# A gated attention block on one core: the main pass's transfers put in written order, the ratios stored in sorted order, and another order of steps in front of the loop

## The chip, the cores and the metric

The kernel runs on one core of one Trainium2 chip. Its time is the device time of one execution in microseconds (us); lower is better. The core has five engines with an instruction queue each: TensorE (PE in the profile; its weight loads are PEld), VectorE (DVE), ScalarE (ACT), GpSimd (POOL) and SyncE (SP). In this kernel SP issues nearly all transfers between memory and the core and does nothing else; what the page calls SPq is SP issuing or waiting.

## What is computed

32 sequences `x` of 256 tokens by 256 channels attend to 32 contexts of 77 tokens, and a feed-forward stage with its own attention follows. All in float32. Cut to what matters:

```python
def proj(t):                                  # layer norm, then 8 heads of 128 features
    return (layer_norm(t, ln_g, ln_b) @ w_in.T) -> [head, batch, token, 128]
f_q, f_k = proj(_layernorm(x)), proj(ctx)     # f_v == f_k
cosine   = f_q . f_k / (|f_q| |f_k|)
q_ratio  = 2 min(var f_q, 1) / (var f_q + 1)  # one number per query and head; k_ratio alike
decorr   = exp(-5 |offdiag(cov f_q)| / D^2)   # one number per head, over all batches
cw, vw, ww = softmax(small_mlp(mean f_q, mean f_k))     # per head, over all batches
mixed    = cw*cosine + vw*decorr*cosine + ww*q_ratio*k_ratio
x = x + tanh(g_xattn) * (mixed @ f_v) @ w_out.T
x = x + tanh(g_ffn)   * ffn(_layernorm(x))    # 16 heads, softmax over the queries, two l2 norms, gelu
```

The weights `cw`, `vw`, `ww` and `decorr` of a head need a pass over all the inputs before the first output can be made.

## The kernel before, in words

**Three stretches.** A first pass reads all inputs once for the statistics that the heads' weights need (up to about 70 us in the profile). A stretch in front of the loop makes the heads' weights and the attention of batches 0 and 1 (to about 150 us). Then a loop, written out in Python for 32 batches, does the rest. In it the list `cycle` (L1470) names what one iteration n does: an entry `(ahead, stage, ...)` runs that stage for batch n + ahead. Batches are in flight up to four ahead: batch n is in its feed-forward attention (`scores`, `exponents`, `mix_values`), batch n + 1 gets its cross attention (`query_scores`, `attend`), batch n + 2 its query features and their transposes, batch n + 3 its inputs' norm and its key features, batch n + 4 is loaded. The last two iterations have lists of their own (`last_but_one`, `last`).

**Orders.** PE, ACT, DVE and POOL are wrapped in `InOrder` (L24 to L32): their instructions run in the order in which the code is written, and every one of them bears line 32 in the profile. The transfers are `nc.sync.dma_start` without the wrapper: their place in SP's queue isn't written down but chosen when the program is built, by a scheduler that plays the program through with estimated times. Once built the order is fixed, and SP runs it in order: a transfer whose input isn't there holds up all that are behind it.

**Turning by way of memory.** From batch 2 on, transposes of 32x32 blocks are made by DVE, and the blocks are put in their places by a store to memory and four reads. So a tile has a store and later reads that must wait for its landing. The pairs of one iteration, with the names that the profile uses:

- queries: `turn_queries` (L583) stores `fd<-fb`, 512 KB for each of two halves t; `fetch_queries` (L592) reads `fqT<-fd` in four parts of 128 KB each. `fqT` has one buffer; PE's `query_scores` (`mm<-fqT,fvT`) needs all eight parts.
- keys: `align_keys` (L337, L341) copies the 77 rows of a batch out of the ring `fvx` into `fv`, in 3 to 5 transfers that depend on where the batch falls in the ring's tiles of 128 rows; `turn_keys` (L407) makes `kb` from `fv` on DVE and stores `kd<-kb`; `fetch_keys` (L416) reads `fvT<-kd`.
- inputs: `transpose_inputs` stores `xd<-xb` (L244) and reads `xq<-xd` four times (L246), one right after the other in the code.
- norms of the keys: `align_norms` copies `nr<-nrx` (L359), stores `nd<-nr` in three parts (L363, L367); `fetch_norms` (L375) reads `rows<-nd`, which POOL's `weigh_keys` turns into `wr`.
- ratios of the queries: `spread_ratios` transposes 128x32 numbers into `rb` on DVE and stores `rc<-rb` (L480, 16 KB); `sort_ratios` (L485) copies `rd<-rc` in memory, in another order (8 KB); `fetch_ratios` spreads `rd` over rows: `re<-rd` (L494) and twice `rqr<-rd` (L503, 256 KB each) with `first`, later `rqr<-re` (L508). POOL's `weigh_ratios` multiplies five blocks of 128x256 of `rqr`, four with a multiply alone and the fifth with a multiply and an add, and DVE adds them to the scores (`s<-mm,wr,rqr`).

Other transfers of an iteration: the load of x (L213), `ff_keep`, which stores `z_kept<-zT` (L799) and `x_kept<-x` (L800) for a repair pass that these inputs don't enter, and the output (`out_dram<-x`, L873, in `ff_add`).

`fb`, the buffer of the transposed queries, and `kb` share two buffers in turn. `keep_running(n)` is n matmuls of 128x128 by 256 columns whose result nobody reads.

Of the kernel before, what the change touches and what calls it, by code (L numbers as in the profile page):

```python
# [15 lines left out]
H = 8  # L16
# [19 lines left out]
def gated_block_kernel(  # L36
# [41 lines left out]

    pe, act, dve, pool = (
# [15 lines left out]
    dve.memset(nhalf, -0.5)  # L95
    phalf = const.tile([H, 1], F32, name="phalf")
# [114 lines left out]
    def load_x(b):  # L211
        xt = pa.tile([P, NT, D], F32, tag="x", name="x", bufs=8)
        nc.sync.dma_start(out=xt, in_=x_v[:, b])  # L213
        return xt
# [15 lines left out]
    def transpose_inputs(b):  # L230
# [13 lines left out]
        nc.sync.dma_start(out=xd, in_=xb.rearrange("p j n a -> p j (n a)"))  # L244
        for j in range(4):
            nc.sync.dma_start(  # L246
                out=k["xq"][32 * j : 32 * j + 32].rearrange("p i t c a -> p i (t c a)"),
                in_=xd[:, j].rearrange("(i p) n -> p i n", p=32),
            )
# [72 lines left out]
    def align_keys(b):  # L322
# [9 lines left out]
        while at < M:  # L332
            i, row = divmod(b * M + at, P)
            n = min(P - row, M - at)
            if at < MA:
                n = min(n, MA - at)
                nc.sync.dma_start(out=k["fv"][at : at + n], in_=fvx[i % 4][row : row + n])  # L337
            else:
                for odd in range(2):
                    to = at + 16 * odd  # L340
                    nc.sync.dma_start(  # L341
# [9 lines left out]
    def align_norms(b):  # L351
# [4 lines left out]
        while at < M:  # L356
            i, row = divmod(b * M + at, P)
            n = min(P - row, M - at)
            nc.sync.dma_start(out=nr[at : at + n], in_=nrx[row : row + n, i % 4, :])  # L359
            at += n  # L360
        k["nd"] = nd = dram.tile([P, 5, 2], F32, tag="nd", name="nd")
        for i in range(2):
            nc.sync.dma_start(  # L363
# [3 lines left out]
        nc.sync.dma_start(  # L367
# [4 lines left out]
    def fetch_norms(b):  # L372
        k = kept[b]
        k["rows"] = pa.tile([P, 5, 2], F32, tag="rows", name="rows")
        nc.sync.dma_start(out=k["rows"], in_=k.pop("nd"))  # L375
# [7 lines left out]
    def turn_keys(b):  # L383
# [23 lines left out]
        nc.sync.dma_start(out=kd, in_=kb.rearrange("p j h a -> p j (h a)"))  # L407
        k["kd"] = kd

    def fetch_keys(b):  # L410
# [4 lines left out]
        for j in range(4):  # L415
            nc.sync.dma_start(  # L416
# [57 lines left out]
    def spread_ratios(b):  # L474
# [4 lines left out]
        k["rc"] = dram.tile([P, 32], F32, tag="rc", name="rc")  # L479
        nc.sync.dma_start(out=k["rc"], in_=rb)  # L480

    def sort_ratios(b):
        k = kept[b]
        k["rd"] = dram.tile([H * NT, 4, 32], F32, tag="rd", name="rd")
        nc.sync.dma_start(  # L485
            out=k["rd"], in_=k.pop("rc").rearrange("(i c) a -> c i a", c=32)[0 : H * NT]
        )

    def fetch_ratios(b, first):
        k = kept[b]  # L490
        if first:
            rd = k.pop("rd")
            k["re"] = dram.tile([P, S], F32, tag="re", name="re")
            nc.sync.dma_start(  # L494
# [6 lines left out]
            for i in range(2):  # L501
                src = rd.rearrange("(g j t) i a -> j g (t i a)", j=2, t=NT)[i]
                nc.sync.dma_start(  # L503
# [3 lines left out]
        else:  # L507
            nc.sync.dma_start(out=k["rq"][:, 4, :], in_=k.pop("re"))  # L508

    def weigh_ratios(b):  # L510

        k = kept[b]
        for g in range(5):
            r = k["rq"][:, g, :]
            if g < 4:
                pool.tensor_scalar(r, r, k["wr"][:, g, 1:2], None, ALU.mult)
            else:
                pool.tensor_scalar(
                    r, r, k["wr"][:, g, 1:2], ident[:, MR + 1 : MR + 2], ALU.mult, ALU.add
                )  # L520
# [37 lines left out]
    def turn_queries(b, t):  # L558
# [24 lines left out]
        nc.sync.dma_start(out=fd, in_=fb.rearrange("p j h a -> p j (h a)"))  # L583
        k["fd", t] = fd

    def fetch_queries(b, t):
# [4 lines left out]
        for j in range(4):  # L591
            nc.sync.dma_start(  # L592
# [203 lines left out]
    def ff_keep(b):  # L796

        k = kept[b]
        nc.sync.dma_start(out=z_kept[:, b], in_=k["zT"])  # L799
        nc.sync.dma_start(out=x_kept[:, b], in_=k["x"])  # L800
# [35 lines left out]
    def mend(b):  # L836
        zT = pa.tile([P, 2, S], F32, tag="zT", name="zT", bufs=1)
        nc.sync.dma_start(out=zT, in_=z_kept[:, bass.ds(b, 1)].squeeze(1))
        xt = pa.tile([P, NT, D], F32, tag="x", name="x", bufs=8)
        nc.sync.dma_start(out=xt, in_=x_kept[:, bass.ds(b, 1)].squeeze(1))  # L840
# [16 lines left out]
        nc.sync.dma_start(out=o_v[:, bass.ds(b, 1)].squeeze(1), in_=xt)  # L857
# [12 lines left out]
    def ff_add(b):  # L870
        u = kept[b]["u"]
        dve.scalar_tensor_tensor(kept[b]["x"], u, tg[:, 1:2], kept[b]["x"], ALU.mult, ALU.add)
        nc.sync.dma_start(out=o_v[:, b], in_=kept[b]["x"])  # L873
        kept[b] = None

    def ff_finish(b):
# [3 lines left out]
        for t in range(NT):  # L880
# [4 lines left out]
            nc.sync.dma_start(out=o_v[:, b, t], in_=x)  # L885
# [16 lines left out]
    def load_w_in(i):  # L902
        nc.sync.dma_start(
# [4 lines left out]
    def load_w_out():  # L908
        nc.sync.dma_start(out=w_out_n, in_=w_out.rearrange("(c p) e -> p c e", p=P))
# [3 lines left out]
    def load_ff(*pairs):  # L913
        for w_t, w in pairs:
            nc.sync.dma_start(out=w_t, in_=w.rearrange("(c p) o -> p c o", p=P))
# [3 lines left out]
    def load_ctx(g):  # L919
        ct = sw.tile([P, 4, D], F32, tag="ct", name="ct", bufs=2)  # L920
        n = min(4, NCTX // P - 4 * g)
        if n > 0:
            nc.sync.dma_start(
# [3 lines left out]
        if n < 4:  # L927
            nc.sync.dma_start(out=ct[0 : NCTX % P, n, :], in_=c_v[(4 * g + n) * P : NCTX])
# [19 lines left out]
    def load_small():  # L948
        nc.sync.dma_start(out=grow, in_=ln_g.partition_broadcast(P))
        nc.sync.dma_start(out=w1_n, in_=wp_w1)  # L950
# [722 lines left out]
```

## Time and profile before

| what | us |
|---|---|
| median of 3 runs (1324.97 to 1327.15) | 1326.67 |
| the profiled execution's own time | 1331.82 |
| its span, first to last instruction | 1330.0 |
| PE busy in the span | 1253.8 (94%) |
| DVE, ACT, POOL busy | 1038.6, 871.3, 643.9 |
| mean granted TensorE clock | 0.982 |
| mean busy share of the 16 DMA engines, from queue q1's packets | 53.5% |

The profile comes from one execution. Busy time is that of an engine's own instructions; matmuls are pipelined, so a busy PE isn't PE at its peak, but a gap between two matmuls is time in which PE did nothing. The view of waits says which engine waited for whom, with the total, the number of times and the longest; the chain of waits is followed back from the last instruction to what released it at each step; the timeline lists instructions in order of time. A transfer's line in the timeline is its issue on SP. Its landing is the last update of the semaphore that it counts on.

### The profile page before, as it was taken

The page shows a single profiled execution, that of the slowest core. Times are in us where ns is not written, and L with a number is a line of the kernel's source. Part 1 is how long each engine was busy: PE and PEld are TensorE (multiplying, and loading weights), DVE is VectorE, ACT ScalarE, POOL GpSimd, SP SyncE. Part 2 cuts the span into 40 slices and gives each one's busy share as a digit, 9 for nine tenths or more (in the row PEclk, how much of TensorE's full clock was granted, in tenths as well). Part 3 has the DMA queues.
Part 4 walks back from the last instruction along what each step waited for, and adds up shares of the span by engine and source line. Part 5 has one row for each costly group of instructions (what it writes and reads, how often), then busy time and mean ns, then how long its engine had stood idle before and what let it go on. Part 6 is the DMA issues. An engine that isn't in the chain of part 4 may idle for free.

```text
span 1330.0 us, 28175 instructions
## 1 busy us (share of the span) xinstructions
PE 1253.8 (94%) x9195; PEld 731.1 (55%) x9195; DVE 1038.6 (78%) x3009; ACT 871.3 (66%) x2826; POOL 643.9 (48%) x785
## 2 busy tenths in 40 slices
PE   8998999999899998999999998999998989999977
PEld 7865555555455554555554554555554545555543
DVE  6845788787788897888887887877796978978845
ACT  6821477677577776666776776765676766767746
POOL 6934554545454554355464454434554544554420
PEclk9998999999899999999999999999999999999989
DMA  8611356655566656456656565553665565464521
GB/s 276 209 37 38 73 137 149 161 152 122 143 146 170 179 144 168 120 155 155 171 116 176 144 170 166 145 125 119 150 164 163 142 176 151 120 157 140 132 61 41
DMA packets 180434, 188.29 MB, mean 142 GB/s; under 512 B 53065, under 2 KB 143358, under 8 KB 180286
## 3 DMA queue, kind: packets, MB, share of 16 engines
q1 hardware_dynamic: 179454, 186.47, 53.5%
q8 instruction: 74, 1.21, 0.5%
q14 instruction: 74, 0.61, 0.2%
q10 hardware_dynamic: 832, 0.00, 0.0%
HBM read 99.43 MB, written 81.17 MB: 136 GB/s over the span
## 4 chain that ended last, share of the span: by engine, by line
PE 68%; DMA 15%; DVE 6%; SPq 4%; issue 2%; POOL 2%; ACT 1%; ACTq 0%; DVEq 0%; POOLq 0%
PE mm L32 52%; PE sc L32 9%; PE zp L32 7%; DMA fqT<-fd 2%; DMA fd<-fb 2%; DMA rqr<-re 2%; DMA rc<-rb 2%; DMA z_kept<-zT 1%; DVE nm L32 1%; SPq L592 1%; DVE qt L32 1%; DMA xq<-xd 1%; ACT e L32 1%; DMA rd<-rc 1%; DVE qst L32 1%
## 5 line engine op out<-in xcount | busy, mean ns | idle before, releaser
L32 ACT ACTIVATE e<-sc,nm 128x256 f32<-128x256 f32 x1016 | 468.9, 487 | 220.1 <-DVE nm L32 220.0
L32 DVE TENSOR_REDUCE nm<-sc 128x4 f32<-128x1024 f32 x254 | 297.9, 1214 | 40.5 <-PE sc L32 39.7
L32 PE MATMUL mm<-winT,xTc 128*128 128x512 f32 x512 | 234.5, 599 | 0.0
L32 ACT ACTIVATION_READ_ACCUMULATOR e<-sc,nm 128x1 f32 x1016 | 221.8, 218 | 0.0
L32 POOL TENSOR_TENSOR rq<-qt,nhalf 128x8 f32<-128x8 f32 x64 | 105.9, 1654 | 106.4 <-DVE qt L32 105.9
L32 POOL TENSOR_SCALAR rqr<-rqr,wr 128x256 f32<-128x256 f32 x128 | 117.1, 934 | 79.7 <-DMA rqr<-rd 68.9
L32 PE MATMUL mm<-vw,s 128*128 128x256 f32 x640 | 149.6, 390 | 4.5 <-DVE s L32 4.5
L32 PEld LDWEIGHTS mm<-winT,xTc 128*128 128x128 f32 x512 | 94.2, 190 | 104.7 <-issue 95.7
L32 PE MATMUL sc<-q,kTf 32*128 32x512 f32 x1016 | 148.6, 642 | 1.2 <-ACT q L32 0.7
L32 PE MATMUL mm<-fqT,fvT 128*32 128x256 f32 (+1 forms) x1536 | 103.8, 425 | 44.1 <-DMA rqr<-re 17.6
L32 PE MATMUL zp<-e,vz 128*32 128x256 f32 x2048 | 137.0, 385 | 4.9 <-DVE vz L32 4.7
L32 PEld LDWEIGHTS mm<-vw,s 128*128 128x128 f32 x640 | 121.1, 193 | 34.0 <-issue 18.2
L32 POOL TENSOR_TENSOR fq<-fq,rq 128x1024 f32<-128x1024 f32 x64 | 121.4, 1898 | 5.0
L32 PEld LDWEIGHTS mm<-fqT,fvT 128*32 128x32 f32 (+1 forms) x1536 | 55.1, 118 | 100.0 <-DVE vz L32 17.5
L32 POOL TENSOR_TENSOR nrx<-kt,nhalf 128x8 f32<-128x8 f32 (+1 forms) x20 | 32.9, 1647 | 153.7 <-DVE kt L32 153.7
L32 DVE BATCH_NORM_STATS2 qst<-fq 128x6 f32<-128x128 f32 x512 | 104.7, 277 | 0.0
L32 PEld LDWEIGHTS zp<-e,vz 128*32 128x32 f32 x2048 | 53.4, 109 | 92.4 <-DVE vz L32 31.6
L32 DVE SCALAR_TENSOR_TENSOR s<-mm,wr,rqr 128x256 f32<-128x256 f32 x160 | 67.9, 477 | 36.9 <-PE mm L32 22.7
L32 POOL TENSOR_SCALAR rs<-mv 128x1 f32<-128x1 f32 x64 | 14.8, 231 | 158.8 <-DVE mv L32 117.7
L32 PE MATMUL mm<-woutT,fvT 128*32 128x256 f32 (+1 forms) x1536 | 89.3, 379 | 1.7 <-DMA fvT<-kd 0.7
L32 PEld LDWEIGHTS sc<-q,kTf 32*128 32x128 f32 x1016 | 41.3, 185 | 75.8 <-issue 33.2
L32 POOL TENSOR_SCALAR xn<-x,mv_x,rstd_x 128x256 f32<-128x256 f32 x64 | 78.8, 1240 | 4.2 <-issue 4.2
(235 smaller groups left out, 2082.9 us busy)
## 6 DMA issues: line engine op xcount, KB each, us to landing
fd<-fb SPq DMA_DIRECT2D x60, 512.0 KB
fqT<-fd SPq DMA_DIRECT2D x240, 128.0 KB
x<-in_x_dram SPq DMA_DIRECT2D x64, 256.0 KB
rqr<-rd SPq DMA_DIRECT2D x64, 256.0 KB
kd<-kb SPq DMA_DIRECT2D x30, 384.0 KB
fvT<-kd SPq DMA_DIRECT2D x120, 96.0 KB
x_kept<-x SPq DMA_DIRECT2D x32, 256.0 KB
z_kept<-zT SPq DMA_DIRECT2D x32, 256.0 KB
```

The lines of the kernel that those rows point to most:

```text
L32: return lambda *args, **kw: self._tc.keep_in_program_order(method(*args, **kw))
L592: nc.sync.dma_start(out=k["fqT"][32 * j : 32 * j + 32, 4 * t : 4 * t + 4].rearrange("p i h a -> p i (h a)"), in_=fd[:, j].rearrange("(i p) ...
```

## The change

**Written order in the loop.** All transfers of SP go through `dma(...)`, which uses `queue[0]`. That is `nc.sync` up to the loop, and `InOrder(tc, nc.sync)` from the loop on: in the loop SP's queue is now in the order in which the code is written.

**Reads apart from their stores.** `transpose_inputs` loses its four reads to a new stage `fetch_inputs`, `align_norms` its three stores to `store_norms`, `ff_keep` is cut in two (0: z, 1: x). `align_keys` moves from batch n + 2 early in an iteration to batch n + 3 late in it; x is kept two iterations earlier, right after `attend`; the queries are fetched at the start of an iteration and no more at the end of the one before.

**Ratios.** `rc` and `sort_ratios` go. `spread_ratios` stores four pieces of 16 rows of `rb` (2 KB each) straight into `rd`. `weigh_ratios` uses multiply and add for all five blocks, with a column of zeros for four of them.

**In front of the loop.** Query statistics and ratios of batch 0 come before the heads' weights are put together, the second halves of batch 1's query features and the turning of its keys come earlier, its key outputs are spread between other steps, and `keep_running(2)` is new.

```diff
+    queue = [nc.sync]
+    def dma(**kw):
+        queue[0].dma_start(**kw)
...
+    zero = const.tile([P, 1], F32, name="zero")
+    dve.memset(zero, 0.0)
...
     def spread_ratios(b):
         rb = pa.tile([P, 32], F32, tag="rb", name="rb")
         dve.transpose(rb, qrs[b % 2])
-        k["rc"] = dram.tile([P, 32], F32, tag="rc", name="rc")
-        nc.sync.dma_start(out=k["rc"], in_=rb)
-    def sort_ratios(b):
         k["rd"] = dram.tile([H * NT, 4, 32], F32, tag="rd", name="rd")
-        nc.sync.dma_start(out=k["rd"], in_=k.pop("rc").rearrange("(i c) a -> c i a", c=32)[0 : H * NT])
+        for i in range(4):
+            dma(out=k["rd"][:, i, :], in_=rb[32 * i : 32 * i + H * NT, :])
...
     def weigh_ratios(b):
         for g in range(5):
             r = k["rq"][:, g, :]
-            if g < 4:
-                pool.tensor_scalar(r, r, k["wr"][:, g, 1:2], None, ALU.mult)
-            else:
-                pool.tensor_scalar(r, r, k["wr"][:, g, 1:2], ident[:, MR + 1 : MR + 2], ALU.mult, ALU.add)
+            one = zero if g < 4 else ident[:, MR + 1 : MR + 2]
+            pool.tensor_scalar(r, r, k["wr"][:, g, 1:2], one, ALU.mult, ALU.add)
...
     run(1, transpose_inputs)
+    run(0, scale_queries, 1)
+    run(0, spread_ratios)
+    run(0, fetch_ratios, True)
+    run(0, fetch_ratios, False)
     hw = sw.tile([H, 1], F32, name="hw")
...
+    run(1, query_features, 0, 0)
+    run(0, turn_keys)
+    run(2, key_features)
     pt = mm_tile()
...
     run(0, weigh_keys)
-    run(1, query_features, 0, 0)
-    run(0, scale_queries, 1)
-    run(0, spread_ratios)
-    run(0, sort_ratios)
-    run(0, fetch_ratios, True)
-    run(0, fetch_ratios, False)
     run(0, weigh_ratios)
-    run(0, turn_keys)
-    run(2, key_features)
...
     run(0, turn_queries, 1)
+    run(1, query_features, 1, 0)
+    run(1, query_features, 1, 1)
     run(2, norm_inputs)
...
     run(0, attend, 1)
-    run(1, query_features, 1, 0)
     run(0, ff_stats, 1)
...
     run(1, weigh_keys)
-    run(1, query_features, 1, 1)
+    run(1, turn_keys)
+    keep_running(2)
     run(0, ff_transpose)
+    run(1, key_outputs, 0)
...
     cycle = [
         (4, load_queries),
-        (1, fetch_ratios, False),
...
         (0, exponents, 0, 0),
-        (2, align_keys),
+        (1, fetch_queries, 0),
+        (1, fetch_ratios, False),
+        (1, fetch_queries, 1),
         (-1, ff_out),
-        (-1, ff_keep),
+        (-1, ff_keep, 0),
         (2, turn_keys),
...
+        (2, fetch_keys),
         (2, count_queries, 0),
-        (2, fetch_keys),
...
         (2, scale_queries, 0),
+        (2, store_norms),
         (3, transpose_inputs),
         (2, fetch_norms),
...
         (0, mix_values, 1),
+        (3, fetch_inputs),
         (1, attend, 0),
         (1, ff_stats, 0),
         (1, attend, 1),
+        (1, ff_keep, 1),
...
         (2, spread_ratios),
         (3, key_features),
         (0, scores, 3),
         (1, ff_transpose),
+        (3, align_keys),
         (0, mix_values, 2),
...
         (2, turn_queries, 0),
-        (2, sort_ratios),
...
         (2, turn_queries, 1),
-        (2, fetch_queries, 0),
         (2, fetch_ratios, True),
-        (2, fetch_queries, 1),
         (0, scale_values, 3),
...
+    queue[0] = InOrder(tc, nc.sync)
     for n in range(-4, B):
```

## The prediction

> **What bounds the kernel now.** First the page: PE is busy 94% of the span, and in the chain that ended last it has 68%, transfers 15%.
>
> ```profile
> PE 1253.8 (94%) x9195; PEld 731.1 (55%) x9195; DVE 1038.6 (78%) x3009; ACT 871.3 (66%) x2826; POOL 643.9 (48%) x785
> ...
> PE 68%; DMA 15%; DVE 6%; SPq 4%; issue 2%; POOL 2%; ACT 1%; ACTq 0%; DVEq 0%; POOLq 0%
> ```
>
> Next the rows of PE, iteration by iteration, each counted from the first matmul of `ff_out` ("phase" 0; a phase below 0 belongs to the iteration before). An iteration without a gap lasts 34.79; five have four more matmuls of key features (36.57). The 28 from 184.9 to 1226.4 last 1041.5, and 23 x 34.79 + 5 x 36.57 = 983.0: **58.5 are lost**. Some 44 are gaps of PE. The other 14 stand in the clock rows: after a gap (or two close ones) of about 3.1 and more the granted clock is 0.50 for 3.4 or 6.8, seven times in the loop, which costs half of that. Nearly all gaps stand ahead of the matmuls `mm<-fqT,fvT`; in the view of waits:
>
> ```profile
> PE mm L32 <- DMA rqr<-re: 17.6, 6, 3.3
> PE mm L32 <- DMA z_kept<-zT: 13.7, 5, 3.9
> PE mm L32 <- DMA out_dram<-x: 9.0, 2, 5.6
> ```
>
> These are transfers issued just behind the `fqT` parts, which is what PE needs. The chain of waits shows what made them late (start, duration):
>
> ```profile
> 688.72 0.21 DVE rb L32
> ...
> 693.50 1.79 DMA rc<-rb
> 695.30 2.02 DMA rd<-rc
> ...
> 697.34 0.69 SPq L494
> ...
> 698.13 3.33 DMA fd<-fb
> ...
> 707.69 3.69 DMA rqr<-re
> 711.38 0.08 issue
> 711.46 2.80 PE mm L32 x48
> ```
>
> The reader is to see that the query stores wait in SP's queue behind the ratios: `rb` is ready at 688.9, its store starts 4.6 later (SP waited for other things), then a second landing, and only then, at 698.1, are stores issued whose `fb` was done at 692.7 and 693.8 by DVE's rows.
>
> Three measures from the trace carry the rest. (1) From the issue of the first query store to the landing of the last `fqT` part: 13.2 (median of 30, 12.6 to 13.8), late or not. (2) To the landing of `z_kept`, with the output and `rqr<-re` between: 14.7. (3) The matmuls come at phase 11.06, and a late part frees them about 0.3 after its landing. So the first store must go out before phase -2.5. Before, it went out between -5.0 and +3.4. In the burst the DMA engines are full, so (1) and (2) are sums of bytes:
>
> ```profile
> 628.00:630.00 2.00, 2.00 (x10) 1.58 (x9) 2.00 (x2) 0.91 (x4) 0.00 (x0) 1.00 1.00 338
> 630.00:632.00 2.00, 2.00 (x6) 0.88 (x5) 1.87 (x3) 2.00 (x11) 0.00 (x0) 1.00 0.95 230
> ```
>
> (The last three columns: clock, DMA share, GB/s.)
>
> **The loop, in written order.** I walk SP's new queue with the rows' issue times.
>
> *Ratios.* `rb` ends at phase -8.31 (-10.03 in the five long iterations). Four stores take the place of one (issue 0.36, landing 2.4), a copy (0.60, 2.1) and the wait between. The page has no such store; `kd<-kb` issues in 0.33, `nd<-nr` in 0.63, so 1.3 to 2.5; I take 1.6, as its form, rows times one run, is nearer to `kd`. They needn't wait for each other: three `nd` stores issued 0.65 apart land within 0.9. The landing is needed 4 later, so two landings in a row leave the path of the query stores.
> The Trainium skill ("DMA: Bandwidth & Descriptors", Rules for kernel authors) speaks against this: many small transfers are to be put together, and the same page gives some 2.0 of fixed cost for each. By it, one after the other, four would take 8, and `rd` would land at phase -0.3 and push everything behind it by some 2.5; the `nd` landings here say that they overlap.
>
> *Keys.* `align_keys` now stands between the ratios and the query stores: 0.6 for a copy of `fv` to row 64, 0.9 for each behind it. 3 copies take 2.4, 4 take 3.0, 5 take 4.2. So the first query store goes out at -8.31 + 1.6 + 2.4 = -4.3, at -3.7 or at -2.5; `fb` is ready at -4.6, so the queue decides.
>
> *Burst.* Behind the two stores come `re`, both `rqr<-rd`, the output (which waits for DVE's add, phase -1.6 to -0.1), the load of x, four parts, `rqr<-re`, four parts. Now output, x and `rqr<-re` lie ahead of the last part. That is the set of measure (2) with x for z, both 256 KB: 14.7, up to 0.6 more as `re` (128 KB in runs like a part's, which add 0.6 each) moves inside. The last part lands at 10.4, 11.0 or 12.2. Against 10.75: no wait, 0.25, 1.45; with 0.6 more 0.25, 0.85, 2.05. In iterations 1 to 28 eleven batches have 3 copies, six have 5, and of those with 4 copies that aren't dealt with next, four lie after a short iteration: 10 to 18, **14** taken.
>
> *Slow copies.* A copy of 64 rows lands in 2.3 to 4.7, mostly, but one of 47 rows in 12.0, of 43 in 10.6, of 41 in 10.0: less some 2.0 for a landing, about 0.2 a row. What is issued behind queues up: with the copy of 43 rows ahead of it, a store of 16 KB took
>
> ```profile
> 917.86 7.48 DMA rc<-rb
> ```
>
> In the new order these copies are issued some 7 later, right ahead of the query stores. For batch 13 (23 and 41 rows) the stores' last share starts at about +5 to +7 and not at -3; DVE waits too, since `kb` takes the buffer that the first query store reads. The same 0.2 a row gives PE 6 for batch 13, 8 for 21 (47 and 17 rows), 2.5 to 5 for 23 (21 and 43), 1.5 and 0.5 for 26 and 31: 18 to 31, **22** taken. Three gaps above 3.1 bring the half clock: **5**.
> The skill has the rule behind this row (same page, Why a DMA increments its semaphore by 16 and not by 1): the engines used are the largest number up to 16 that divides the outer count, so 41, 43 and 47 rows run on one engine. It fits the landings. By it 23 rows of batch 13 are on one engine as well, which is the upper end of my term.
>
> *The rest of an iteration.* `kd` is stored after the burst, at about 7, lands near 12; `fvT` is issued by 14.4, lands by 17 to 18, needed at 24.6. `nd` goes out by 16.3, lands by 21; `rows` is behind it, needed at 29.4. SP then waits for `nd` with `xq` and `x_kept` queued: `xq` lands by 26, POOL needs it at 29.6. x is kept at 23.3, SP is free for `rb` at 26.5. Cover of 3 and more each: cost nothing. If `nd` took 5 longer, `rb`'s stores would start late and the burst with them.
>
> *POOL.* Multiply and add costs 570 ns, multiply alone 934 (page):
>
> ```profile
> L32 POOL TENSOR_SCALAR rqr<-rqr,wr,ident 128x256 f32<-128x256 f32 x32 | 18.2, 570 | 0.4 <-DMA rqr<-re 0.4
> ```
>
> Four blocks save 1.5 an iteration beside PE; POOL is on 2% of the chain: nothing in the loop. The memset of zeros and two more transfers an iteration are beside PE too.
>
> Loss in the loop after: 14 + 22 + 5 = 41, from 58.5: **-17.5**. In iteration 30 PE waits 5.65 in a list where the matmuls come earlier; the store goes out at the same -4, so it stays (+-0.5).
>
> **In front of the loop.** PE has one large gap, 119.0 to 123.5, for the ratios, and then 6.8 of half clock (3.4). `rb` came at 109.9, behind the heads' weights; now DVE reaches it 2.1 earlier. Two landings become one (-2.3), three more issues (+1.2), and POOL saves 1.5, this time on the path: `s` is some 4.7 earlier. PE reaches it later, because 8 matmuls of batch 1 (3.9) go ahead. Gap and half clock go: -7.9. Against it `keep_running(2)` 0.8 (390 ns each), and about 1 where `ff_transpose` waits for `xf` without those 8 matmuls beside it. **-6** (-3 to -8).
>
> **Sum.** 1331.8 - 17.5 - 6.2 = 1308 for an execution such as the profiled one, which stands 5.2 above the median shown; against the median, 1326.7 - 23.7 = **1303**.
>
> **Rivals.**
> *The burst fits.* For: most of the bytes ahead of the parts go out in time. If measure (2) comes out at 14.2 and the slow copies cost half, the loss is 5 + 12 + 2 = 19 and the time 1326.7 - 39.5 - 6.2 = 1281.
> *The change moves the wait only.* For: the engines are full in the burst, and bytes went ahead of the parts. At 15.5 from store to last part the short waits grow to about 25, slow copies to 27, clock to 8: 60. The gain is the front's alone or none: 1322 to 1328.
> *Slower.* Output and x ahead of `fqT`: one mechanism, in the queue between `rqr<-rd` and the first part. For: the output waits for DVE, and seven parts and `rqr<-re` wait behind. At 16.2 the sum is 37 (short) + 30 + 10 = 77: 1326.7 + 18.5 - 6.2 = 1339. It decides from about 15.7, 1.0 above what I take. Against: `z_kept` and the output add 0.6 each behind the parts, x has the same size.
> *The order is the old one.* If the scheduler's queue were the written one already, nothing would change; against it, SP's rows show `fqT` ahead of the output, and `fv` in other places from one iteration to the next.
>
> **Chances.** Forecast 0.50 (1290 to 1318), burst fits 0.24, moved 0.12, slower 0.14. Eight in ten: 1280 to 1330, with the first rival's time in it and the slower one's out. 0.2% is about what a measurement of this kernel can tell from no change: faster 0.50 + 0.24 + 0.03 of "moved" = 0.77, same 0.07, slower 0.14 + 0.02 = 0.16.
>
> **What would show it.** Right: the first query store at -4.3 to -2.5 in every iteration; 14.7 to 15.3 from it to the last `fqT` part; gaps ahead of `mm<-fqT,fvT` under 2 except for batches 13, 21 and 23 (iterations 11, 19, 21), where they are 3 to 9; no gap of 4.5 near 120. Wrong: stores later than -2.5 throughout, a burst longer than 15.7, or PE waiting at another place, such as `mm<-woutT,fvT` (keys too late).

## The result, and the profile after

Of nine executions each on one chip, before took 1324.97 us in the median (1317.88 to 1327.43) and the changed kernel 1316.39 (1312.90 to 1325.85); the ratio is 0.9944, with a 95% interval of 0.9917 to 0.9972. So the change makes the kernel faster by some 0.6%, where 1.8% was forecast. The profiled execution of the changed kernel took 1316.39, with a span of 1314.5 and a mean granted clock of 0.992.

The span is 15.5 shorter than the one of before, more than the medians differ, as the profiled execution of before stood above its own median. From the rows of PE: the first pass, to the last `sc<-xna`, took 1.5 more; from there to the first `ff_out` of the loop 108.0 in place of 114.3; iterations 1 to 28 lose 49.2 in place of 58.5; what follows took 1.4 less. The nine executions of before have a median 6.9 under the profiled one. If all of that is the loop's, a median loop of before loses some 52 (an estimate: 58.5 less 6.9). Then of the 8.6 by which the medians differ the front has 6.3 and the loop only 2 to 3.

First the page of the changed kernel, with its line on engines, the chain that ended last, and four rows of its groups (busy time, mean ns of one, idle time ahead of it and what ended most of that).

```profile
PE 1244.4 (95%) x9199; PEld 728.4 (55%) x9199; DVE 1034.2 (79%) x3010; ACT 871.5 (66%) x2826; POOL 594.3 (45%) x785
...
DVE 0%; DVEq 0%; issue 0%
...
L32 PE MATMUL mm<-vw,s 128*128 128x256 f32 x640 | 146.7, 384 | 0.0
L32 PE MATMUL zp<-e,vz 128*32 128x256 f32 x2048 | 137.9, 387 | 8.5 <-DVE vz L32 8.2
L32 PE MATMUL mm<-fqT,fvT 128*32 128x256 f32 (+1 forms) x1536 | 94.3, 396 | 37.8 <-DVE qt L32 12.7
...
L32 POOL TENSOR_SCALAR rqr<-rqr,wr,zero 128x256 f32<-128x256 f32 x128 | 69.1, 552 | 23.3 <-DMA rqr<-rd 23.2
```

The chain was lost at the last instruction here and says nothing. The same two rows of PE on the page of before:

```profile
L32 PE MATMUL mm<-vw,s 128*128 128x256 f32 x640 | 149.6, 390 | 4.5 <-DVE s L32 4.5
...
L32 PE MATMUL mm<-fqT,fvT 128*32 128x256 f32 (+1 forms) x1536 | 103.8, 425 | 44.1 <-DMA rqr<-re 17.6
```

The row of `mm<-vw,s` had 4.5 idle before: the gap for the ratios in front of the loop is gone. The row of `mm<-fqT,fvT` had 44.1 and still has 37.8. The mean matmul in it took 425 ns and now takes 396: less of it runs at half clock.

The view of waits (total, times, longest) shows how the loss has changed its form:

```profile
PE mm L32 <- DVE qt L32: 12.7, 9, 1.8
PE zp L32 <- DVE vz L32: 8.2, 3, 4.5
PE mm L32 <- DMA kd<-kb: 6.9, 5, 2.8
...
PE mm L32 <- DMA z_kept<-zT: 6.4, 3, 3.2
```

Before, there were few waits and long ones. Now there are many of 1 to 2 us. The names at the right (DVE's `qt`, `kd<-kb`, `z_kept<-zT`) are only what happened last when the matmul could start; the matmuls are the same, and what they need are the `fqT` parts: at each of the 22 gaps ahead of them they start 0.1 to 0.5 after the last part has landed. In sum PE stands still for about as long as before: all its gaps in the 28 iterations come to 41.0, where they came to 44.2. What else has gone of the loss is half clock.

SP's timeline for the burst of one iteration (start, duration, count) shows the new queue:

```profile
207.78 1.71 SPq L32 DMA_DIRECT2D rd<-rb  x4
209.53 3.75 SPq L32 DMA_DIRECT2D fv<-fvx  x5
213.37 0.86 SPq L32 DMA_DIRECT2D fd<-fb  x2
214.28 0.72 SPq L32 DMA_DIRECT2D re<-rd  x1
215.09 1.86 SPq L32 DMA_DIRECT2D rqr<-rd  x2
217.04 0.55 SPq L32 DMA_DIRECT2D out_dram<-x  x1
217.64 0.42 SPq L32 DMA_DIRECT2D x<-in_x_dram  x1
218.17 2.01 SPq L32 DMA_DIRECT2D fqT<-fd  x4
220.22 0.43 SPq L32 DMA_DIRECT2D rqr<-re  x1
220.91 3.00 SPq L32 DMA_DIRECT2D fqT<-fd  x4
```

All eight parts are issued within 10.5 of the first store, and the last lands 15.3 after it, at phase 12.6. From 220 on the DMA engines are full; the three stretches of 2 us before have shares of 0.89, 0.91 and 0.66 (last two columns: DMA share and GB/s):

```profile
220.00:222.00 2.00, 2.00 (x12) 0.69 (x10) 1.97 (x5) 2.00 (x11) 2.00 (x2) 1.00 1.01 328
222.00:224.00 2.00, 2.00 (x25) 0.72 (x18) 1.97 (x3) 0.54 (x2) 1.83 (x4) 1.00 1.15 215
224.00:226.00 2.00, 2.00 (x6) 0.95 (x5) 2.00 (x7) 2.00 (x9) 2.00 (x4) 1.00 1.08 183
```

Medians over the 28 iterations, before and after: the first query store goes out at phase -1.6 (-5.0 to +3.4) and now at -3.4 (-4.9 to -1.4), as written; but the last part lands 13.2 after it before and 15.4 now, so at 11.4 before and at 12.2 now. PE wants it by 10.75. Before, 14 of 28 landings were later than that, some by 5; now it is 26, most of them by less than 2.

### The profile page after: what moved, and what is told of

Its sections match the earlier page's. It is cut to its first block, busy times and chain, and to the rows that moved or that the text cites. A ratio compares the mean times of both kernels' runs of the same rounds, so it can differ in the third digit from the quotient of the medians.

```text
span 1314.5 us, 28234 instructions
## 1 busy us (share of the span) xinstructions
PE 1244.4 (95%) x9199; PEld 728.4 (55%) x9199; DVE 1034.2 (79%) x3010; ACT 871.5 (66%) x2826; POOL 594.3 (45%) x785
## 5 line engine op out<-in xcount | busy, mean ns | idle before, releaser
L32 PE MATMUL mm<-vw,s 128*128 128x256 f32 x640 | 146.7, 384 | 0.0
L32 PE MATMUL mm<-fqT,fvT 128*32 128x256 f32 (+1 forms) x1536 | 94.3, 396 | 37.8 <-DVE qt L32 12.7
L32 PEld LDWEIGHTS zp<-e,vz 128*32 128x32 f32 x2048 | 53.6, 109 | 96.0 <-DVE vz L32 24.4
L32 PEld LDWEIGHTS sc<-q,kTf 32*128 32x128 f32 x1016 | 40.5, 183 | 74.4 <-issue 38.5
L32 POOL TENSOR_SCALAR rqr<-rqr,wr,zero 128x256 f32<-128x256 f32 x128 | 69.1, 552 | 23.3 <-DMA rqr<-rd 23.2
```

What stands on the lines that cost most here:

```text
L32: return lambda *args, **kw: self._tc.keep_in_program_order(method(*args, **kw))
```

## The experiments

Each kernel is the changed one with the edit that is shown, and runs beside the kernel before on the same chip. Chips differ (before took 1335.9, 1323.8 to 1324.1 and 1322.2 on three of them), so ratios are compared. The columns: ratio to before with its interval; then from the profile, in us, the phase of the first query store, the time from it to the last `fqT` landing, the phase of that landing (medians of 28), the loss of iterations 1 to 28, and the front (last `sc<-xna` to the loop). A profile is one execution. Those of before, a0 and e5 took 6 to 7 more than the median of their kernel, those of e4 and e9 4.2 less, the others lie within 2.5 of it; so losses that stand this close together tell no two kernels apart.

| kernel | ratio to before | store | to landing | lands | loss | front |
|---|---|---|---|---|---|---|
| before | 1 | -1.6 | 13.2 | 11.4 | 58.5 | 114.3 |
| the change | 0.9944 (0.9917 to 0.9972) | -3.4 | 15.4 | 12.2 | 49.2 | 108.0 |
| e0, before again | 1.0007 (0.9982 to 1.0032) | -1.5 | 13.2 | 11.7 | 64.4 | 113.6 |
| a0, the change again | 0.9950 (0.9931 to 0.9969) | -3.2 | 15.4 | 12.2 | 57.0 | 106.7 |
| e2, x behind | 0.9784 (0.9765 to 0.9803) | -3.5 | 14.6 | 11.2 | 31.3 | 108.0 |
| e3, x and output behind | 0.9590 (0.9545 to 0.9634) | -3.4 | 13.8 | 10.5 | 19.5 | 107.0 |
| e1, keys early | 0.9589 (0.9549 to 0.9630) | -4.6 | 15.3 | 10.7 | 16.4 | 108.2 |
| e4, copies cut | 0.9913 (0.9876 to 0.9951) | -3.0 | 15.4 | 12.5 | 53.3 | 108.4 |
| e4b, the same again | 0.9940 (0.9915 to 0.9965) | -2.8 | 15.2 | 12.1 | 46.1 | 106.7 |
| e5, scheduler's order | 0.9990 (0.9961 to 1.0019) | -2.6 | 13.6 | 10.8 | 60.4 | 110.9 |
| e9, ratios in two steps | 0.9874 (0.9806 to 0.9942) | -4.6 | 15.6 | 11.2 | 38.5 | 106.7 |
| e8, multiply alone | 0.9935 (0.9905 to 0.9965) | -3.3 | 15.4 | 12.1 | 53.7 | 108.0 |
| e10, old front | 0.9987 (0.9955 to 1.0018) | -3.4 | 15.7 | 12.4 | 59.5 | 107.7 |
| e6, e1 + e3 + e4 | 0.9561 (0.9542 to 0.9580) | -4.6 | 13.4 | 8.7 | 0 | 108.2 |
| e11, e6 with the old front | 0.9573 (0.9554 to 0.9593) | -4.6 | 13.6 | 8.9 | 0 | 107.7 |
| e12, e6 with two steps | 0.9570 (0.9551 to 0.9589) | -4.6 | 13.8 | 9.0 | 0 | 107.9 |
| e13, e1 + e3 | 0.9604 (0.9580 to 0.9628) | -4.6 | 13.4 | 8.8 | 2.6 | 106.7 |
| e14, e6 without filler | 0.9564 (0.9544 to 0.9583) | -4.6 | 13.4 | 8.6 | 0 | 108.0 |

### The two kernels again

> The kernel before, unchanged, for a second profile. In the first one the 28 loop iterations lost 58.5 us against 34.79 (36.57 for the five long ones). If that is the kernel's usual loss, this profile shows 55 to 62 again. If the first profile caught a bad execution (it stood 5 above the median), it shows 45 to 55, and part of my miss was the base and not the new order.

> The changed kernel itself, unaltered, beside the three variants that follow. Theory (the miss is a burst of 15.4 us from the first query store to the last query part, where 14.7 was taken): ratio to before 0.985 to 0.996, the loop loses 46 to 54 us against iterations without gaps, the store's issue to the last landing is 15.2 to 15.5 in the median. Rival (the small gain was chance of one profiled execution): the loop loses under 44, or the ratio is below 0.982.

The ratios and the bursts come out as they were; both losses lie above the ranges given. A single execution scatters: the loop of the changed kernel lost 49.2 in one profile and 57.0 in the other, that of before 58.5 and 64.4, for a good part by how often a gap brings the half clock (8.2 and 13.6 of the changed kernel's two losses aren't gaps). The time from the first store to the last landing is the firm number: 15.36 and 15.39.

### What lies ahead of the last query part

> The load of x (256 KB) is issued behind the eight query parts in place of ahead of them; the output stays ahead. Theory that the burst is a sum of bytes: store to last part falls from 15.4 by 256 KB at some 290 GB/s, 0.9, to 14.5; nearly all short waits shrink by as much, 28 iterations lose 27 to 34 in place of 49, ratio to the changed kernel 0.985 to 0.990. Rival that it is the output's wait for DVE's add that holds the parts (all bytes being moved alike): store to last part 15.2 to 15.4, ratio 0.997 to 1.003.

```diff
     cycle = [
-        (4, load_queries),
...
         (1, fetch_queries, 1),
+        (4, load_queries),
```

The theory of bytes fits, the rival falls: 256 KB less ahead of the last part take 0.8 from the burst (15.39 in a0, 14.57 here). The loss falls from 57.0 to 31.3 and the time by 1.7% (0.9784 beside 0.9950), a little more than expected.

> The changed kernel with the load of x and the store of the output moved behind the eight parts of fqT. Theory A: 0.65 us of transfer work each no longer lie ahead of the last part, which lands 14.0 to 14.2 after the first query store instead of 15.4; short waits from 27 to 4 to 10, slow copies unchanged; loss from 49 to 25 to 32, time 1292 to 1302. Rival C (eight transfers in flight: the last part waits for the first part's landing, so only the first part's issue counts): the first part goes out 3.5 after the first store, 0.5 to 1.5 earlier than now, and the last part lands 9.6 after it, the same gain or up to 0.5 more. Rival D (PE waits for something of DVE, as the view of waits names it): nothing changes.

```diff
     def ff_add(b):
...
-        dma(out=o_v[:, b], in_=kept[b]["x"])
+    def ff_store(b):
+        dma(out=o_v[:, b], in_=kept[b]["x"])
...
         (1, fetch_queries, 1),
+        (-2, ff_store),
+        (4, load_queries),
```

With the output behind as well it is 13.79, a little less than theory A put: again 0.8 for 256 KB. So the output costs what x costs, with DVE's add or without it, and rival D falls too. Rival C can't be told from the theory of bytes. Of SP's transfers eight are under way at most, and in the change, in e2 and in e3 the last part is issued 0.02 after the landing of the first part, which is eight transfers before it (medians of 28). With x and the output behind, the first part goes out 3.8 after the first store in place of 4.9, and the last lands 9.9 after that in place of 10.3; C had put 3.5 and 9.6. Whether it is the bytes in full engines or the eight places that set the 0.8 stays open. The page of e3, rows of two kinds of matmuls, `zp` and those that need the query parts:

```profile
L32 PE MATMUL zp<-e,vz 128*32 128x256 f32 x2048 | 138.8, 389 | 8.6 <-DVE vz L32 8.4
L32 PE MATMUL mm<-fqT,fvT 128*32 128x256 f32 (+1 forms) x1536 | 91.2, 386 | 10.6 <-DMA out_dram<-x 6.0
```

37.8 of idle time has become 10.6. What stays is the wait of `zp`, that of two batches with slow copies.

> The changed kernel with key features and key copies moved ahead of the ratios in the list, so the copies go out some 5 us earlier; PE, DVE, ACT and POOL keep their orders. Theory A (the new losses are late query stores plus a burst of 15.4 us): the first query store goes out at phase -4.5 in every iteration, the short waits (27 us in all) fall to 3 to 8, the waits behind slow copies (batches 13, 21, 23, 26; 20 us with the half clock) to 2 to 8; loss of iterations 1 to 28 from 49 to 5 to 16, time 1275 to 1288. Rival B (the bytes and the output's wait on DVE decide, not the store's start): the last part stays at 11.5 to 12.5, loss 40 to 50, time within 6 of the changed kernel.

```diff
+        (3, key_features),
+        (3, align_keys),
         (2, scale_queries, 1),
         (2, spread_ratios),
-        (3, key_features),
...
-        (3, align_keys),
```

Here the burst keeps its bytes (15.3), and the key copies go ahead of the ratios' stores, out of the space between these and the query stores. The first store goes out 1.2 earlier and the last part lands 1.5 earlier. That is worth as much as 512 KB less. Start and bytes are two ends of one sum.

### The slow copies

> The changed kernel with each key copy to row 64 cut into a piece of a multiple of 16 rows and the rest; 47 rows become 32 + 15. Theory A (the copies of 41, 43, 47 rows are slow because of their row count, and all transfers behind them queue up): these copies land in 2.3 to 4.5 instead of 10 to 12, the waits of iterations 11, 19, 21 and 24 fall from 20 to 4 to 8, while one or two more issues of 0.6 delay the query store in 11 iterations (+3 to +6 short waits): loss from 49 to 36 to 42. Rival E (the copies are slow because they queue behind other transfers): their landing and the four iterations stay as they are, loss 50 to 55.

> A copy of key features whose rows aren't a multiple of 16 is cut into a multiple of 16 and a rest, nothing else. Theory that the slow copies cost what iterations 11, 12, 19, 21 and 24 lose above the others (24.7, less 5 ordinary ones of 1.2: some 18): ratio to the unaltered changed kernel 0.986 to 0.989. Rival that the time saved there comes back, since each cut adds an issue ahead of the query stores and the start slips by 0.4 to 0.6 in the other batches: these five lose 8 to 15 in all, the other 23 lose 34 to 40 in place of 24, and the ratio is 0.995 to 1.005.

```diff
-                dma(out=k["fv"][at : at + n], in_=fvx[i % 4][row : row + n])
+                n16 = n // 16 * 16
+                if n16:
+                    dma(out=k["fv"][at : at + n16], in_=fvx[i % 4][row : row + n16])
+                if n > n16:
+                    dma(out=k["fv"][at + n16 : at + n], in_=fvx[i % 4][row + n16 : row + n])
```

In iteration 11 of the changed kernel the copy of 41 rows is issued at 534.66 and lands 13.9 later, at 548.56. SP's timeline shows what that does to the queue:

```profile
533.84 3.28 SPq L32 DMA_DIRECT2D fv<-fvx  x4
537.22 0.93 SPq L32 DMA_DIRECT2D fd<-fb  x2
538.24 1.10 SPq L32 DMA_DIRECT2D re<-rd  x1
539.39 3.18 SPq L32 DMA_DIRECT2D rqr<-rd  x2
548.62 0.34 SPq L32 DMA_DIRECT2D out_dram<-x  x1
549.00 0.43 SPq L32 DMA_DIRECT2D x<-in_x_dram  x1
550.06 2.20 SPq L32 DMA_DIRECT2D fqT<-fd  x4
```

Nothing is issued from 542.57 to 548.62. The output takes the semaphore that the copy had eight transfers before, and goes out 0.06 after its landing. The first `fqT` part goes out 8 us into the iteration.

What makes these copies slow stands in the updates of their semaphores in the trace. The copy of 41 rows and one of 23 rows, issued just ahead of it, raise theirs twice each, once early and once at their landings, which come one behind the other (540.73 and 548.56). In e6 a copy of 32 rows raises it 16 times and one of 9 rows 10 times. Rival E of e4 falls: cut, and at the same place in the queue, the copies land early.

Cut at multiples of 16, no such copy lands later than 3.2 after its issue (e4b; 4.2 in e4), and iterations 11, 12, 19, 21 and 24 lose 13.8 (14.5 in e4) in place of 24.7 to 25.7. But the ratio is that of the uncut version, as the rival of e4b said: the others lose 32.3 (38.8 in e4) in place of 24.4 to 31.3, as each cut is one more issue of 0.5 to 0.9 ahead of the query stores (first store at -2.8 in place of -3.2 to -3.4). What is saved in five iterations comes back in the others, in part or in whole.

> Keys early, x and output behind the query parts, but the copies not cut. Theory (the two edits in the order take every wait but the slow copies' of batches 13 and 21, which the first edit alone left at 2.5 and 7.7): iterations 11 and 19 lose 5 to 10 together, all others under 1 each, ratio to the version with all three 1.004 to 1.008. Rival (with 1.6 less in the burst the slow copies are covered too): the loop loses under 2, ratio under 1.002.

Neither holds in the profile. Without the cut the copies land up to 12.6 after their issue here too, but the two iterations lose 0.9 and 1.7, where they lose 5.4 and 6.9 in the changed kernel and 2.5 and 7.7 in e1. The profiled execution is the fastest of four, though; the median is some 3 us above those of its neighbours e11, e12 and e14 (1268.68 beside 1264.86 to 1265.53), and the ratio to e6, 1.0045, is the theory's. With room in the burst most of a slow copy is covered.

### The parts of the change by themselves

> The one line that puts SP's queue into written order is left out; the lists, the stages and the four stores of the ratios stay as in the changed kernel. Theory (the order keeps the first query store between -4.9 and -1.4; left to the scheduler it spreads from -5 to +3 as before): the loop loses 52 to 70 us where the changed kernel loses 49, ratio to before 0.997 to 1.008. Rival (the moved stages alone bring the gain and the written order costs it back, since the scheduler puts output and x behind the query parts): the loop loses under 40, ratio to before under 0.988.

```diff
-    queue[0] = InOrder(tc, nc.sync)
```

Left to the scheduler, the first store spreads from -5.7 to +2.5 again, the parts land 13.6 after it, and the loop loses 60.4, as the theory said. The view of waits shows them as long as before's:

```profile
PE mm L32 <- DMA kd<-kb: 20.5, 6, 4.3
PE mm L32 <- DMA z_kept<-zT: 15.0, 6, 5.0
```

So the written order brings the first store forward and narrows its spread, and it makes the burst 1.8 longer; the one takes back most of the other. Whether the loop gains by it at all isn't shown: the profiles of e5 and a0, both 6 to 7 above their medians, lose 60.4 and 57.0, and of the 7.6 between the two medians the front has 4.2.

The shorter burst also bounds the theory of bytes. In 27 of its 28 iterations the output stands ahead of the last part here, and in all of them `rqr<-re`, 384 KB together; x goes out behind, and `re` ahead of the first store, as before. At 0.8 for 256 KB that would be 1.2 more than before's 13.2; it is 0.4. So 0.8 is the price in the change's own order, and not for every queue. (The front is 3 longer here: its transfers come in another order as well, and a gap of 3.5 ahead of `mm<-ident,fq` brings a half clock.)

> The ratios go by a store of 16 KB and a sorting copy again, in the place of the four stores; the copy stands behind the first query store. Theory (four issues cost SP 1.3 to 1.6 ahead of the key copies, the two landings now stand beside the query stores): first query store 0.9 to 1.2 earlier, the reads of the ratios wait for the copy by up to 1, the last part lands between 0.6 earlier and 0.4 later, ratio to the changed kernel 0.990 to 1.004. The first matmul of the loop comes 1 to 2 later. Rival (two landings in a row hold the queue, and the four stores carry the change's gain): last part over 1 later in the median, the loop loses over 70, ratio to the changed kernel above 1.012.

```diff
-        for i in range(4):
-            dma(out=k["rd"][:, i, :], in_=rb[32 * i : 32 * i + H * NT, :])
+        k["rc"] = dram.tile([P, 32], F32, tag="rc", name="rc")
+        dma(out=k["rc"], in_=rb)
+    def sort_ratios(b):
+        dma(out=k["rd"], in_=k.pop("rc").rearrange("(i c) a -> c i a", c=32)[0 : H * NT])
...
         (2, turn_queries, 0),
+        (2, sort_ratios),
```

The store is 1.2 earlier, the last part 1.05 earlier, more than the theory gave, the loss 38.5 (in an execution 4.2 faster than the median), and the front no longer than with the four stores (106.7). The four stores cost time in this loop: that is read from the trace, as the intervals of the two ratios overlap.

> The version with all three edits, with the ratios' store and sorting copy in the place of the four stores. Theory (in a loop without waits neither form is on the path; the last query part lands over 1 ahead of its need): loop loses 0 to 1, first query store no later, ratio 0.998 to 1.001. Rival (two landings in a row): the reads of the ratios wait, the last part lands after 10.75 in some batches, the loop loses 5 or more, ratio above 1.004.

Once the loop has no waits, either form gives the same time (1265.53 beside 1264.86 and 1265.42 of e14 and e11, which have the four stores and ran on the same chip).

> GpSimd multiplies four of five blocks with a multiply alone again (934 ns in place of 552). Theory (beside PE in the loop, on the path once in front of it): the loop's loss stays within 5 us, its first matmul comes up to 1.5 later, ratio to the changed kernel 0.998 to 1.004. Rival (the blocks are ready 1.5 later for the scores of every iteration, and PE waits): the loop loses 20 or more above the changed kernel, ratio above 1.012.

The loss of 53.7 lies between the changed kernel's two, the front is 108.0: the faster operation brings nothing that can be measured.

> The order of steps in front of the loop is that of before, the loop and the four stores are those of the changed kernel. Theory (the gap of 4.5 and its half clock come back, less a landing that the stores save): the first matmul of the loop comes at 183 to 185 in place of 180.1, the loop is the same, ratio to the changed kernel 1.002 to 1.004. Rival (the four stores and the faster multiplies make the gain in front, not the order): first matmul at 180 to 182, ratio within 0.002 of 1. A third (a late front shifts nothing, as a later wait takes it up): first matmul later, total the same.

> The version with all three edits, with the order of steps in front of the loop as before. Its loop has no waits, so that the front stands alone. Theory (the four stores and the faster multiplies alone shorten the gap of 4.5 below the point from which the clock halves; the new order of steps is worth its last 1.4, less what the filler and the later waits cost): the first matmul of the loop at 177.5 to 180, the loop loses 0 to 1, ratio to the version with all three 0.999 to 1.001. Rival (the new order is worth the 5 us by which the two totals with and without it stood apart): ratio 1.003 to 1.005, in the front's rows or in the loop's.

```diff
     run(1, transpose_inputs)
-    run(0, scale_queries, 1)
-    run(0, spread_ratios)
-    run(0, fetch_ratios, True)
-    run(0, fetch_ratios, False)
...
     run(0, weigh_keys)
+    run(1, query_features, 0, 0)
+    run(0, scale_queries, 1)
+    run(0, spread_ratios)
+    run(0, fetch_ratios, True)
+    run(0, fetch_ratios, False)
     run(0, weigh_ratios)
+    run(0, turn_keys)
+    run(2, key_features)
...
-    run(1, turn_keys)
-    keep_running(2)
+    run(1, query_features, 1, 1)
```

The page's row for the gap in front of the loop, of e10:

```profile
L32 PE MATMUL mm<-vw,s 128*128 128x256 f32 x640 | 146.7, 384 | 1.4 <-DVE s L32 1.4
```

With the steps in the old order the four stores and the faster multiplies alone shorten the gap from 4.5 to 1.4; no half clock follows, and the front is 107.7, as short as with the new order, which has other gaps in its place (`mm<-ident,fq` waits 1.4 and 0.8 for POOL). In e11, where the loop has no waits, the ratio is 0.9573 beside 0.9561 of e6, with intervals that overlap. In e10 the loop lost 59.5, more than in either profile of the changed kernel, and its median is 5.5 above a0's. Why an order in front of the loop should make the loop's burst 0.3 longer stays open; e11 shows only that it costs nothing that can be measured where the burst has room.

> The version with all three edits, without the two matmuls of filler in front of the loop. Theory (the filler is 2 x 390 ns of PE on the path): first matmul of the loop 0.5 to 0.8 earlier, ratio 0.9993 to 1.0. Rival (the filler keeps the gap ahead of it under the length from which the clock halves): a gap above 3.1 or a half clock between 125 and 150, first matmul 1 to 3.5 later.

The gap at that place is 1.1, no half clock follows, and the front is 108.0 beside 108.2 of e6: nothing is seen of the filler's 0.8 in either direction.

### All three edits

> Three edits together: key features and their copies ahead of the ratios' stores, x and the output behind the query parts, copies cut at multiples of 16 rows. Theory (start of the stores and bytes ahead of the last part add up): store at -5.7 or -4.6, last part 13.6 to 13.8 later, at phase 8 to 9.2, ahead of 10.75 in every batch; slow copies gone; the loop loses 1 to 6 us and the time is 1266 to 1274, ratio to before 0.948 to 0.954. Rival (one wait hides another, so that two edits that each give 33 us give the same 33 together): 1278 to 1284, ratio 0.957 to 0.961, with PE waiting for keys or for DVE's feature work in place of the query parts.

The page of e6, its line on engines and the row of the matmuls that need the query parts, then a burst in SP's timeline:

```profile
PE 1235.4 (98%) x9199; PEld 717.4 (57%) x9199; DVE 1027.7 (81%) x3010; ACT 871.4 (69%) x2826; POOL 595.6 (47%) x785
...
L32 PE MATMUL mm<-fqT,fvT 128*32 128x256 f32 (+1 forms) x1536 | 91.9, 388 | 4.5 <-DMA out_dram<-x 4.5
```

```profile
205.36 1.72 SPq L32 DMA_DIRECT2D rd<-rb  x4
209.08 1.46 SPq L32 DMA_DIRECT2D fd<-fb  x2
210.72 0.68 SPq L32 DMA_DIRECT2D re<-rd  x1
211.50 1.32 SPq L32 DMA_DIRECT2D rqr<-rd  x2
212.91 1.97 SPq L32 DMA_DIRECT2D fqT<-fd  x4
214.97 0.38 SPq L32 DMA_DIRECT2D rqr<-re  x1
215.39 2.17 SPq L32 DMA_DIRECT2D fqT<-fd  x4
217.98 0.36 SPq L32 DMA_DIRECT2D out_dram<-x  x1
218.64 0.35 SPq L32 DMA_DIRECT2D x<-in_x_dram  x1
```

There is 2.0 between the ratios' stores and the query stores in which SP waits for `fb`: now DVE sets the start, and no longer the queue (the store goes out 0.03 after `fb` ends, in 26 of 28 iterations). All 28 iterations last 34.79 or 36.57 to within 0.12; the 4.5 that is left is the wait of iteration 30. The time is 1265.57 (1262.54 to 1267.03), a little under what the theory gave, and the loss is under it too, 0 for 1 to 6; the ratio to before, 0.956, is just above its 0.948 to 0.954. The ratio to the changed kernel on the same chip is 0.961 (1265.57 by 1316.64). The edits add up until no wait is left.

## Why the prediction was wrong, step by step

**The size of the burst is the step that failed.** The prediction took the set of its measure (2), with x for z, at "14.7, up to 0.6 more". It measured 15.4. The runs take this apart: 13.2 before, with neither `re` nor `rqr<-re`, output or x between the first store and the last part; 13.8 in e3, with `re` and `rqr<-re` between them; 14.6 in e2, with the output too; 15.4 with x. The prediction priced 256 KB at 0.6, by transfers that stand behind the parts in before; ahead of the parts, in this order, output and x cost 0.8 each. And it took the lower end of its own 14.7 to 15.3.

**The short waits follow from it.** The last part was put at 10.4, 11.0 and 12.2 for 3, 4 and 5 key copies. It lands at 11.3, 12.0 and 12.7 (medians of 11, 7 and 5 iterations). The store went out at -4.0, -3.4 and -2.6, against -4.3, -3.7 and -2.5 foretold, so 0.3 of it is the start with 3 and 4 copies and nothing with 5; the rest is the burst. With the need at 10.75, the landings had been put within 1.5 of it, so that 0.5 to 1.0 more on each nearly doubles the term: iterations other than 11, 12, 19, 21 and 24 lose 24.4, and 31.3 in a0, where 14 was taken. In the profiled execution that is 10.4 more, less 2.3 that the slow copies cost less: the 8.2 by which the loss of 49.2 exceeds the forecast of 41.

**The base.** The prediction worked out a loss for the loop after (41) and took its difference to the loss of a profiled execution that stood 5.2 above the median shown; then it took this difference from the median. A median execution of before had less to lose. Of the 13.4 by which the time was missed (1316.4 for 1303), 5.2 is this; the other 8.2 is the loop's. Against the nine executions of before (1324.97) the forecast gain of 23.7 stands beside 8.6, and the part of the base is 6.9.

**Right.** The slow copies and their half clock (22 + 5): the five iterations lose 24.7 and 25.7, partly by DVE's wait ahead of `zp`. The size has some luck in it: in the profiled execution 17.9 are gaps and 6.8 half clock, and 4.5 belong to iteration 12, which wasn't named; its store is the latest of all (-1.4), right behind the late iteration 11. The Trainium skill (DMA: Bandwidth & Descriptors, Why a DMA increments its semaphore by 16 and not by 1) has the rule, that the number of engines must divide the outer count, and the trace agrees: the copy of 41 rows raises its semaphore twice and lands after 13.9; in e6, where it goes as 32 and 9 rows, these raise it 16 and 10 times and land after 2.3 and 2.5. The rest of an iteration has its cover: `mm<-woutT,fvT` waits for nothing (1.7 before). GpSimd's operation takes 552 ns and is off the path (e8). Iteration 30 keeps its wait, 4.6 in place of 5.65.

**The front: right sum, wrong account.** -6.2 was foretold, -6.3 measured (-6.9 from e0 to a0). The prediction added up the order of steps, the stores and the multiplies. e10 and e11 show that the stores and multiplies are enough, and e8 and e9 that the order is enough without one or the other of them: as far as these profiles tell, it is enough that the gap falls to where no half clock follows it. Of the filler, costed at 0.8, e14 finds nothing.

**The ratios.** Four issues were put at 1.6 and took 1.7, their landings overlapped (1.4 each in the median), as argued from the `nd` stores. (The 2.0 that was set against this, from the skill's page, is fitted there to transfers on GpSimd's path; these are SP's, and didn't land one after the other.) But the prediction counted the landing that went off the path as the gain, and SP's time as small. In this loop it is the other way about: the sorting copy stands where SP has room, the four issues stand ahead of the query stores (e9). The skill's rule on small transfers (same page, Rules for kernel authors) pointed the right way; its reason, overhead of each transfer, shows here as issue time in the queue.

**The rivals.** What happened is nearest to "the change moves the wait only", which put 15.5 and a loss of 60; 15.4 and 49 to 57 were measured, and most of the gain is the front's, as it said; only its time, 1322 to 1328, lies above the 1316.4. "Slower" would have needed 15.7 or more. "The burst fits" is what e1 and e3 make of the change, with 16 to 20 lost. "The order is the old one" is out: e5 differs from the change in just that line, and its stores spread from -5.7 to +2.5.

## What to carry to other kernels

Where many transfers go out together and one reader waits for the last, write down the sum: when the first can start, and how many bytes stand ahead of the last one that somebody needs; then move what nobody waits for behind it, and what is only in the way of the start ahead of it. When waits are near zero, a term of 0.7 in every iteration is worth more than the few long gaps that a profile shows first, so price a full stretch by rows in which the same transfers stand at the same place, and not by the nearest total. And take the base of a difference from the same execution as the difference.

## What the runs showed that had not been expected

- SP's transfers take eight semaphores in turn in this program, and one waits to be issued for the landing of the one eight before it: 6.0 us of SP's queue stood still for one copy of 41 rows (164 KB).
- Ahead of the last query part 256 KB cost 0.8, whether they are read or written (x in e2, the output in e3), but in the order of e5 384 KB cost 0.4.
- The half clock has no sharp edge. The prediction put it at gaps of about 3.1. In the loops of eight profiles (before, e0, the change, a0, e4, e4b, e5, e10) with one gap over 0.3 in an iteration, none of 96 gaps below 2.1 brought it, 27 of 47 between 2.1 and 3.6 did, and all 4 above. That is the larger part of why one kernel's loop loses 49 in one execution and 57 in the next at the same length of its bursts (5.4 of 7.8; gaps are the rest). Without waits, the loops of e6, e11, e12 and e14 lose the same to 0.1.
